# GraphSAGE layer ends: the last half in two groups of blocks, statistics gathered ahead, and the next layer's first h written by two engines

## The chip, the cores and the metric

The kernel runs on one core of one Trainium2 chip. A core has a matrix engine (PE; its weight loads are listed as PEld), a vector engine (DVE), a scalar engine (ACT), a general engine (POOL) and a queue engine that only starts transfers (SP). The matrix engine writes its results into PSUM, a memory[...], and transfers (DMA) go between SBUF and device memory. The metric is the device time of one execution in microseconds, as the median of several runs.

## The reference, cut to what matters

An attention layer comes first and is not touched. The second part is a three-layer GraphSAGE over 16 graphs of 1024 nodes with 128 features:

```python
def _sage(x, adj, Wr, Wx, b, mf):
    deg = jnp.clip(jnp.sum(adj, axis=-1, keepdims=True), 1.0, None)
    agg = jnp.einsum('bij,bjd->bid', adj, x) / deg
    out = agg @ Wr + x @ Wx + b
    nrm = jnp.maximum(jnp.linalg.norm(out, axis=-1, keepdims=True), NORM_EPS)
    return out / nrm * mf[..., None]

def _bn(x, g, b):
    m = jnp.mean(x, axis=(0, 1))
    v = jnp.var(x, axis=(0, 1))
    return (x - m) * jax.lax.rsqrt(v + BN_EPS) * g + b

h1 = _bn(jax.nn.relu(_sage(x, adj_d, Wr1, Wx1, b1, mf)), g1, be1)
h2 = _bn(jax.nn.relu(_sage(h1, adj_d, Wr2, Wx2, b2, mf)), g2, be2)
h3 = _bn(jax.nn.relu(_sage(h2, adj_d, Wr3, Wx3, b3, mf)), g3, be3)
xc = jnp.concatenate([h1, h2, h3], axis=-1) * mf[..., None]
return (xc @ Wl + bl) * mf[..., None]
```

`_bn` takes its mean and variance over all graphs and all nodes. So nothing of layer L + 1 can be computed before the last node of layer L is done, and the scale and shift of the batch norm ("affine") stand between the two layers.

## The kernel before, in words

Each layer goes through the 16 graphs `b`, and each graph through two halves `c` of 512 nodes (512 = 4 blocks of 128). One half is one call of the generator `nodes(L, b, c, hT, aT)`. Here `hT` is the layer's input, features on the partitions; `aT` the masked adjacency for this half; `ys[b % 2]` the product of the input with Wr, made by `given`.

A half goes like this. PE makes `own` = bias + h Wx, and ACT copies it into `mine` (L1123). Then for each of the four blocks `i`, PE adds up eight 128x128 products into `pg` (L1132). `pg` is one PSUM tile of shape [P, 2, 512], that is two banks: blocks 0 and 1 lie in the first bank, blocks 2 and 3 in the second. In layer 0 column 128 of each block carries the node degree. After the fourth block, DVE takes all four together: in layer 0 the degree and its reciprocal (L1143, L1146), then `o = pg * rdeg + mine`, one instruction for each block (L1150). ACT squares `o` (L1155), DVE adds the squares up per row (L1158) and bounds them (L1160), ACT takes the root (L1161), DVE the reciprocal, the mask and relu times 1/norm (L1163 to L1165). PE transposes the result into the bank `pt` (L1169), ACT copies it to `hTs[b]`, which stays in SBUF (L1173), and DVE takes batch-norm statistics of it (`bn_stats`, L1176, or L1172 in a layer's last half): mean and variance of 512 columns for each feature, one of 32 entries in `late["stats"]`.

The order of the instructions on PE, ACT and DVE is written out by hand: the block runs under `tc.manual_schedule`, and each of these engines executes in program order. The generator's `yield`s let the main loop interleave two halves: while PE makes the sums of half `this`, DVE and ACT do the steps "scaled", "norm", "result", "transposed" and "end" of the half `before` (L1256 to L1313). Beside them, DVE applies the dilation masks to the `aT` of the next half: four `pieces` of 1.2 us each, made by `masks` (L146). SP's and POOL's queues are filled by the scheduler. On SP stand the loads of `aT` (2 MB, four buffers) and of the mask's data `mr` (two of 0.5 MB for each half, four buffers); a load waits until its buffer is free, and holds what is queued behind it. On POOL stand the loads and stores of the output's accumulator (`sums_so_far` and L1069).

A tile that two engines access is guarded by semaphores that the framework sets. PSUM tiles come by tag: `bank` with "n" gives the one bank for `given`, "t" the one for transposes, "g" half of a two-bank tile out of the same two slots that `pg` uses.

At a layer's end (L1318 to L1336) nothing is left to interleave: the last half goes through "scaled" to "end" alone. In layers 1 and 2 PE has the output products of the previous layer for graphs 14 and 15 to do there (`last_parts`, 4 parts of 8 products; L1059), and DVE their 16 additions afterwards (L1064). Then `bn_aggr` joins the 32 entries (L1325), and six small operations give `affine` (L1328 to L1332). The next layer begins at L1220: ACT writes `h` of graph 0 in two halves (`incoming`, L1096), PE makes `given` for each (L1103; both use the bank "n", so the second waits for ACT's copy of the first, L1105), then `own` and the sums of the first half. After layer 2 the output loop follows (L1388 to L1406): `come` applies the last batch norm, `products` multiplies by Wl's third part (L1364), DVE and ACT add the rows to the accumulator (L1372, L1401, L1385), and SP stores the result. Its products for graphs with b % 4 < 2 go into one two-bank tile, for the others into two single banks (L1355 to L1359).

Of the kernel before, what the change touches and what calls it, by code (L numbers as in the profile page):

```python
# [10 lines left out]
F32 = mybir.dt.float32  # L11
# [4 lines left out]
AF = mybir.ActivationFunctionType  # L16
ALU = mybir.AluOpType
# [4 lines left out]
P = 128  # L22
LN_EPS = 1e-5
BN_EPS = 1e-5
NORM_EPS = 1e-12
# [9 lines left out]
def swept(ctx: ExitStack, tc: tile.TileContext, t: dict, out: bass.AP, flag: bass.AP):  # L35
# [8 lines left out]
    nc = tc.nc  # L44
    x, adj, nodemask = t["x"], t["adj"], t["nodemask"]
    B, N, D = x.shape
# [3 lines left out]
    HB = NB // 2  # L50
    HN = N // 2

    const = ctx.enter_context(tc.tile_pool(name="const", bufs=1))
# [7 lines left out]
    ident = const.tile([P, P], F32, name="ident")  # L61
# [17 lines left out]
    def last(ap, d):  # L79

        return ap.unsqueeze(2).to_broadcast([P, ap.shape[-1], d])
# [69 lines left out]


    mf2 = const.tile([P, B * NB], F32, name="mf2")
    bn_eps = const.tile([P, 1], F32, name="bn_eps")
    nc.vector.memset(bn_eps, BN_EPS)
    minus_half = const.tile([P, NB], F32, name="minus_half")
    nc.vector.memset(minus_half, -0.5)

# [931 lines left out]
    def incoming(L, b, c, hT, affine):  # L1090

        if L == 0:
            whole(incoming_first(L, b, c, hT))
        else:
            cc = slice(c * HN, (c + 1) * HN)
            nc.scalar.activation(hT[:, cc], hTs[b][:, cc], AF.Identity, bias=affine[:, 1:2], scale=affine[:, 0:1])  # L1096

    def given(L, b, c, hT, tag="n"):

        pn = bank(f"pn_{L}_{b}_{c}", tag).rearrange("p (k d) -> p k d", d=D)  # L1100
        for i in range(HB):
            n = (c * HB + i) * P
            nc.tensor.matmul(pn[:, i, :], hT[:, n : n + P], wts[f"Wr{L + 1}"], start=True, stop=True)  # L1103
        yield "evict"
        nc.scalar.copy(ys[b % 2][:, c * HB : (c + 1) * HB, :D], pn)  # L1105

    def nodes(L, b, c, hT, aT):

        y = ys[b % 2]
        k0 = b * NB + c * HB
        width = D + 1 if L == 0 else D
        own = bank(f"own_{L}_{b}_{c}", "o").rearrange("p (k d) -> p k d", d=D)
        start_with(own, 2 + L, P)
        for i in range(HB):
            n = (c * HB + i) * P
            nc.tensor.matmul(own[:, i, :], hT[:, n : n + P], wts[f"Wx{L + 1}"], start=False, stop=(i == HB - 1))
        yield "own"

        def evict():
            mine = late["pool"].tile([P, HB, D], F32, name=f"mine_{L}_{b}_{c}", tag="mine")
            nc.scalar.copy(mine, own)  # L1123
            return mine


        mine = evict() if late else None
        pg = ps_s.tile([P, 2, 512], F32, name=f"pg_{L}_{b}_{c}", tag="sc")
        for i in range(HB):
            for j in range(NB):  # L1130
                at = (i % 2) * (D + 1)
                nc.tensor.matmul(  # L1132
                    pg[:, i // 2, at : at + width], aT[:, j, i * P : (i + 1) * P], y[:, j, :width],
                    start=(j == 0), stop=(j == NB - 1),
                )
            yield "sums"
        if not mine:
            mine = evict()
            yield "mine"
        pool, small, rdeg = late["pool"], late["small"], late["rdeg"]  # L1140
        if L == 0:
            dg = rdeg[:, k0 : k0 + HB]
            nc.vector.tensor_scalar(  # L1143
                dg.rearrange("p (q i) -> p q i", q=2), pg[:, :, D : 2 * D + 2 : D + 1], 1.0, None, ALU.max
            )
            nc.vector.reciprocal(dg, dg)  # L1146
        o = pool.tile([P, HB, D], F32, name=f"o_{L}_{b}_{c}", tag="o")
# [17 lines left out]
        nc.vector.scalar_tensor_tensor(o, o, 0.0, last(f, D), ALU.max, ALU.mult)  # L1165
        yield "result"
        pt = bank(f"pt_{L}_{b}_{c}", "t")
        for i in range(HB):
            nc.tensor.transpose(pt[:, i * P : (i + 1) * P], o[:, i, :], ident)  # L1169
        last_half = b == B - 1 and c == 1  # L1170
        if last_half:
            nc.vector.bn_stats(late["stats"][:, 2 * b + c, :], pt)  # L1172
        nc.scalar.copy(hTs[b][:, c * HN : (c + 1) * HN], pt)  # L1173
        yield "transposed"
        if not last_half:
            nc.vector.bn_stats(late["stats"][:, 2 * b + c, :], pt)  # L1176
        yield "end"

    turns = [(L, b, c) for L in range(3) for b in range(B) for c in range(2)]

# [4 lines left out]
    def go(steps, *names):  # L1185
        for name in names:
            assert next(steps) == name


    late = {}  # L1190
    hTs = []
# [13 lines left out]
        late["rdeg"] = late["small"].tile([P, B * NB], F32, name="rdeg", bufs=1)  # L1205

    def new_stats(L):
        late["stats"] = late["small"].tile([P, 2 * B, 6], F32, name=f"stats{L}", tag="stats", bufs=2)

    p1 = ctx.enter_context(ExitStack())  # L1210
    affine = None
    with tc.manual_schedule(
# [3 lines left out]
        hT, last_rows = attend()  # L1216
        next(last_rows)
        nothing = lambda: None
        for L in range(3):
            if L > 0:  # L1220
                new_stats(L)
                hT = shared.tile([P, N], F32, name=f"h_{L}_0", tag="ad", bufs=2)
                for c in range(2):
                    incoming(L, 0, c, hT, affine)
                for c in range(2):
                    whole(given(L, 0, c, hT))
            before = None

            held, last_parts = ["o", "g", "g", "y"], []
            for b in range(B):  # L1230
# [4 lines left out]
                for c in range(2):  # L1235
# [49 lines left out]
                            next(last_rows)  # L1285
                    if biased:
                        next(biased)
                    turn_later = before and (c == 0 or L == 0)
                    if before and not turn_later:
                        go(before, "transposed")  # L1290
                    pieces[2]()
                    pieces[3]()
                    if before and not turn_later:
                        go(before, "end")
                    go(this, "sums")
                    if turn_later:
                        go(before, "transposed", "end")
# [17 lines left out]
                    fetch_h0(b + 2)  # L1315
                if more:
                    hT = hTn
            go(before, "scaled")  # L1318
            for part in last_parts[:2]:
                next(part)  # L1320
            go(before, "norm", "result", "transposed", "end")
            for part in last_parts[2:]:
                next(part)
            mv = late["small"].tile([P, 3], F32, name=f"mv{L}", tag="mv", bufs=2)
            nc.vector.bn_aggr(mv[:, 0:2], late["stats"])  # L1325

            affine = late["small"].tile([P, 2], F32, name=f"affine{L}", tag="affine", bufs=2)
            nc.scalar.activation(mv[:, 1:2], mv[:, 1:2], AF.Sqrt, bias=bn_eps)  # L1328
            nc.vector.scalar_tensor_tensor(mv[:, 2:3], mv[:, 0:1], -1.0, late["norms"][:, L, 0:1], ALU.mult, ALU.mult)
            nc.vector.reciprocal(mv[:, 1:2], mv[:, 1:2])  # L1330
            nc.vector.tensor_tensor(affine[:, 0:1], late["norms"][:, L, 0:1], mv[:, 1:2], ALU.mult)
            nc.vector.scalar_tensor_tensor(  # L1332
                affine[:, 1:2], mv[:, 2:3], mv[:, 1:2], late["norms"][:, L, 1:2], ALU.mult, ALU.add
            )
            for part in last_parts:
                whole(part)  # L1336

# [4 lines left out]
                nc.sync.dma_start(tile_[:, b], acc_d[1][4 * i + b])  # L1342
            outs.append(tile_)


        hs = {}

        def come(b):
            if b < B:
                hs[b] = shared.tile([P, N], F32, name=f"h_3_{b}", tag=("ad", "xin")[b % 2], bufs=2 + b % 2)  # L1350
                for c in range(2):
                    incoming(3, b, c, hs[b], affine)
# [625 lines left out]
```

## Time and profile before

| | |
|---|---|
| median of 3 runs | 3398.19 us (3393.63 to 3403.14) |
| profiled execution | 3396.91 us, span 3395.1 us |
| PE, DVE, ACT busy over the span | 98%, 89%, 68% |
| mean granted PE clock | 0.995 |
| DMA | 772.28 MB, mean 227 GB/s |
| last half of layers 0, 1, 2: sums end, affine ready | 2649.37, 2657.74; 2994.93, 3002.98; 3336.34, 3344.39 us |
| next layer's (or output's) first product of that kind | 2664.96; 3007.82; 3346.60 us |

Times are from the start of the span. "Granted clock" is the share of the full rate that the matrix engine was given. The three GraphSAGE layers lie from 2326 us to 3345 us of the span, and the three layer ends lie at about 2650, 2995 and 3336 us. In a timeline row, the numbers are start and length, then engine, source line, operation, output and input with sizes, how many instructions were merged, and in brackets how long the engine had been idle before it and which instruction ended the wait.

### The profile page before, as it was taken

The page shows a single profiled execution, that of the slowest core. Times are in us where ns is not written, and L with a number is a line of the kernel's source. Part 1 is how long each engine was busy: PE and PEld are TensorE (multiplying, and loading weights), DVE is VectorE, ACT ScalarE, POOL GpSimd, SP SyncE. Part 2 cuts the span into 40 slices and gives each one's busy share as a digit, 9 for nine tenths or more (in the row PEclk, how much of TensorE's full clock was granted, in tenths as well). Part 3 has the DMA queues.
Part 4 walks back from the last instruction along what each step waited for, and adds up shares of the span by engine and source line. Part 5 has one row for each costly group of instructions (what it writes and reads, how often), then busy time and mean ns, then how long its engine had stood idle before and what let it go on. Part 6 is the DMA issues. An engine that isn't in the chain of part 4 may idle for free. (4 is left out here: it accounts for less than half of the span.)

```text
span 3395.1 us, 86338 instructions
## 1 busy us (share of the span) xinstructions
PE 3310.6 (98%) x34855; PEld 1872.4 (55%) x34855; DVE 3025.5 (89%) x5399; ACT 2305.4 (68%) x3909; POOL 164.2 (5%) x253
## 2 busy tenths in 40 slices
PE   8999999999999999999999999999999899999997
PEld 3333333333333333333334334336999899999997
DVE  7898989989989998998998999897888899988887
ACT  7699689779879969968976986884232344423334
POOL 2000000000000000000000000000000000000000
PEclk9999999999999999999999999999999999999999
DMA  7357456547637736845863773677999799989996
GB/s 242 108 168 206 137 149 199 161 129 221 188 122 213 221 122 183 238 144 158 236 190 122 237 240 119 189 228 261 346 341 343 284 353 350 353 323 350 352 351 222
DMA packets 650123, 772.28 MB, mean 227 GB/s; under 512 B 173264, under 2 KB 569168, under 8 KB 637424
## 3 DMA queue, kind: packets, MB, share of 16 engines
q1 hardware_dynamic: 632672, 708.58, 64.4%
q0 software_dynamic: 15456, 57.30, 5.0%
q8 instruction: 275, 4.51, 0.6%
q14 instruction: 136, 1.11, 0.1%
q10 hardware_dynamic: 1584, 0.79, 0.1%
HBM read 508.50 MB, written 157.29 MB: 196 GB/s over the span
## 5 line engine op out<-in xcount | busy, mean ns | idle before, releaser
L603 DVE TENSOR_TENSOR w<-e,aT 128x1024 f32<-128x1024 f32 x1024 | 1205.5, 1219 | 138.4 <-ACT e L598 136.8
L598 ACT ACTIVATE e<-sc 128x1024 f32<-128x1024 f32 x1024 | 991.9, 1022 | 333.6 <-PE sc L560 332.6
L1132 PE MATMUL pg<-y,aT 128*128 128x128 f32 (+1 forms) x6144 | 729.8, 275 | 0.0
L1132 PEld LDWEIGHTS pg<-y,aT 128*128 128x128 f32 x6144 | 707.9, 192 | 0.0
L487 PE MATMUL acc<-w,both 128*32 128x512 f32 x4096 | 586.7, 605 | 3.1 <-DVE w L603 2.6
L560 PE MATMUL sc<-qT,kT 32*128 32x512 f32 x4096 | 584.4, 640 | 0.3 <-ACT qT L315 0.3
L492 PE MATMUL acc<-e,eps 128*32 128x512 f32 x4096 | 573.1, 592 | 0.0
L146 DVE SCALAR_TENSOR_TENSOR aT<-mr,aT 128x1024 f32<-128x1024 bf16 x384 | 458.8, 1217 | 0.0
L492 PEld LDWEIGHTS acc<-e,eps 128*32 128x32 f32 x4096 | 150.6, 110 | 294.6 <-issue 289.6
L1155 ACT ACTIVATE sq<-o 128x512 f32<-128x512 f32 x96 | 60.6, 631 | 328.5 <-DVE o L1150 328.5
L554 PEld LDWEIGHTS <-never 32*32 32x32 bf16 x8192 | 80.9, 88 | 347.9 <-issue 325.6
L554 PE MATMUL sc<-nomask,never 32*32 32x512 bf16 x8192 | 252.3, 385 | 16.8 <-ACT e L598 12.3
L1173 ACT COPY hT<-pt 128x512 f32<-128x512 f32 x96 | 56.3, 586 | 289.3 <-PE pt L1169 280.0
L560 PEld LDWEIGHTS sc<-qT,kT 32*128 32x128 f32 x4096 | 160.1, 183 | 116.9 <-issue 116.1
L505 PEld LDWEIGHTS pa<-ident,a 128*128 128x128 f32 x1024 | 107.7, 141 | 181.4 <-issue 129.7
L487 PEld LDWEIGHTS acc<-w,both 128*32 128x32 f32 x4096 | 92.8, 108 | 156.2 <-issue 65.4
L915 ACT ACTIVATE wr<-both,th 128x512 f16<-128x512 f16 x256 | 172.1, 730 | 7.1 <-DVE both L900 6.9
L505 PE MATMUL pa<-ident,a 128*128 128x128 f32 x1024 | 168.3, 287 | 6.4 <-DMA a<-in_adj 5.7
L512 ACT ACTIVATE nomask<-aT 128x512 bf16<-128x512 f32 x256 | 161.4, 630 | 8.1
L1150 DVE SCALAR_TENSOR_TENSOR o<-pg,rdeg,mine 128x128 f32<-128x128 f32 x384 | 108.1, 344 | 55.9 <-PE pg L1132 52.6
L508 ACT COPY aT<-pa 128x512 f32<-128x512 f32 x256 | 152.7, 597 | 5.3 <-PE pa L505 4.3
L900 DVE TENSOR_TENSOR_SCAN both<-rk 128x513 f16<-128x513 bf16 x128 | 155.9, 1218 | 0.0
(228 smaller groups left out, 3894.9 us busy)
## 6 DMA issues: line engine op xcount, KB each, us to landing
aT<-aT_d SPq DMA_DIRECT2D x94, 2048.0 KB, 9.9
mr<-mr_d SPq DMA_DIRECT2D x188, 512.0 KB, 6.0
aT_d<-aT SPq DMA_DIRECT2D x256, 256.0 KB, 4.0
a<-in_adj SPq DMA_DIRECT2D x253, 256.0 KB, 3.7
ad<-in_adj SPq DMA_DIRECT2D x112, 512.0 KB, 4.2
nomask<-nomask SPq DMA_DIRECT2D x512, 96.0 KB, 2.7
nomask<-nomask SPq DMA_DIRECT2D x512, 64.0 KB, 2.7
nomask<-nomask SPq DMA_DIRECT2D x512, 32.0 KB, 2.7
```

Source lines behind the costliest of these rows:

```text
L146: nc.vector.scalar_tensor_tensor(part, mrs[h][:, j : j + 2, :].rearrange("p j n -> p (j n)"), 0.0, part, ALU.is_equal, ALU.mult)
L487: nc.tensor.matmul(acc[g][32 * j : 32 * j + 32, :], v1[:, m, (2 * j + g) * HW : (2 * j + g) * HW + 32], ws[j // 2][:, j % 2, :], start=(m ...
L492: nc.tensor.matmul(acc[g][32 * j : 32 * j + 32, :], eps8, es[j // 2][:, j % 2, :], start=False, stop=(m == NB - 1),)
L505: nc.tensor.transpose(pa[:, k * P : (k + 1) * P], a[:, k, :], ident)
L512: nc.scalar.activation(nomask[:, 0, :], aT[:, 0, :], AF.Relu, bias=1.0, scale=-1e38, accum_out=zeros[:, i : i + 1])
L554: nc.tensor.matmul(scs[j // 2][to : to + 32, j % 2, :], never[rows, rows], nomask[rows, j, :], start=True, stop=False, tile_position=(32 * ...
L560: nc.tensor.matmul(scs[j // 2][:, j % 2, :], kT[rows, mm], qTs[c][rows, g, :], start=False, stop=True, tile_position=(32 * j, 0),)
L598: nc.scalar.activation(e, scs[q], AF.Exp, scale=1.0 / math.sqrt(HD))
L603: nc.vector.tensor_tensor(w, es[q], aT.to_broadcast([P, 2, HN]), ALU.mult)
L900: nc.vector.tensor_tensor_scan(pair_sums[b % 2], row[:, 0::2], row[:, 1::2], 0.0, ALU.add, ALU.add)
L915: nc.scalar.activation(wrs[b][:, t * HN : (t + 1) * HN], pair_sums[b % 2][:, t : t + HN], AF.Abs, bias=at[:, b : b + 1], scale=2.0,)
L1132: nc.tensor.matmul(pg[:, i // 2, at : at + width], aT[:, j, i * P : (i + 1) * P], y[:, j, :width], start=(j == 0), stop=(j == NB - 1),)
```

## The change

The last half of a layer (b = 15, c = 1) leaves the common path. A new generator `ending` takes its four blocks in two groups. The code of the first group (scale, square, norm, relu of blocks 0 and 1) is issued between the sums of block 1 and those of block 2; the scaling of block 2 between the sums of blocks 2 and 3; the rest after block 3. Squares and their sums are made on DVE by one instruction with an accumulator output, and in layer 0 the degree is taken for each block alone. The statistics of the last half go into two entries of their own (`late["two"]`). The 31 other entries are aggregated ahead of the last half's first group (`most`), and the two sets are joined by their weights, 31/32 and 1/32, after the last statistics.

The half before the last one is transposed, copied and put into the statistics before the last half's third block; and the masks `pieces[2:]` of the next half are kept (`owed`) and applied after the next layer's first h. That first h is written by `arrive`: two quarters by ACT, the second half by DVE. In layers 0 and 1 this stands at the head of the next layer, after the additions of `last_parts`; in layer 2 it stands ahead of them. At the end of layer 0, where there are no output products, PE makes 14 and 18 transposes of the identity that nobody reads (`running`).

```diff
+    def arrive(hT, b, affine):
+        for cc in (slice(0, HN // 2), slice(HN // 2, HN)):
+            nc.scalar.activation(hT[:, cc], hTs[b][:, cc], AF.Identity, bias=affine[:, 1:2], scale=affine[:, 0:1])
+        nc.vector.tensor_scalar(hT[:, HN:], hTs[b][:, HN:], affine[:, 0:1], affine[:, 1:2], ALU.mult, ALU.add)
...
             yield "sums"
+            if last_half and i == 1:
+                end = ending(L, k0, pg, mine)
+                go(end, "first group")
+            if last_half and i == 2:
+                go(end, "third block")
+        if last_half:
+            yield from end
+            return
...
+    def ending(L, k0, pg, mine):
...
+        def scaled(i):
+            at, dg = (i % 2) * (D + 1), rdeg[:, k0 + i : k0 + i + 1]
+            if L == 0:
+                nc.vector.tensor_scalar(dg, pg[:, i // 2, at + D : at + D + 1], 1.0, None, ALU.max)
+                nc.vector.reciprocal(dg, dg)
+            nc.vector.scalar_tensor_tensor(
+                o[:, i, :], pg[:, i // 2, at : at + D], dg, mine[:, i, :], ALU.mult, ALU.add
+            )
+            nc.vector.scalar_tensor_tensor(
+                sq[:, i, :], o[:, i, :], 1.0, o[:, i, :], ALU.mult, ALU.mult, accum_out=f[:, i : i + 1]
+            )
+
+        def root(two):
+            nc.vector.tensor_scalar(f[:, two], f[:, two], NORM_EPS**2, None, ALU.max)
+            nc.scalar.activation(f[:, two], f[:, two], AF.Sqrt)
+
+        def normed(two):
+            nc.vector.reciprocal(f[:, two], f[:, two])
+            nc.vector.tensor_tensor(f[:, two], f[:, two], mf[:, k0 + two.start : k0 + two.stop], ALU.mult)
+            nc.vector.scalar_tensor_tensor(o[:, two, :], o[:, two, :], 0.0, last(f[:, two], D), ALU.max, ALU.mult)
+
+        def turned(two):
+            for i in range(two.start, two.stop):
+                nc.tensor.transpose(pt[:, i * P : (i + 1) * P], o[:, i, :], ident)
+
+        def counted(two):
+            nc.vector.bn_stats(late["two"][:, two.start // 2, :], pt[:, two.start * P : two.stop * P])
+
+        first, second = slice(0, 2), slice(2, 4)
+        for i in range(2):
+            scaled(i)
+        root(first)
+        normed(first)
+        yield "first group"
+        scaled(2)
+        yield "third block"
+        pt = bank(f"pt_{L}_end", "t")
+        turned(first)
+        scaled(3)
+        root(second)
+        counted(first)
+        normed(second)
+        yield "result"
+        turned(second)
+        counted(second)
+        nc.scalar.copy(hTs[B - 1][:, HN:], pt)
+        yield "end"
+
+    def running(L, n):
+
+        idle = bank(f"idle_{L}_{n}", "n")
+        for i in range(n):
+            nc.tensor.transpose(idle[:, (i % HB) * P : (i % HB + 1) * P], ident, ident)
...
-                for c in range(2):
-                    incoming(L, 0, c, hT, affine)
+                arrive(hT, 0, affine)
+                for piece in owed:
+                    piece()
...
-                    turn_later = before and (c == 0 or L == 0)
+                    last_half = b == B - 1 and c == 1
+                    turn_later = before and (c == 0 or L == 0) and not last_half
...
+                    if last_half:
+                        owed = pieces[2:]
                         go(before, "end")
+                        most = late["small"].tile([P, 4], F32, name=f"most{L}", tag="most", bufs=2)
+                        nc.vector.bn_aggr(most[:, 0:2], late["stats"])
+                        nc.vector.tensor_scalar(most[:, 2:3], most[:, 0:1], SHARE, None, ALU.mult)
+                        nc.vector.tensor_scalar(most[:, 3:4], most[:, 1:2], SHARE, BN_EPS, ALU.mult, ALU.add)
...
-            go(before, "scaled")
+            go(before, "result")
             for part in last_parts[:2]:
                 next(part)
-            go(before, "norm", "result", "transposed", "end")
+            if L == 0:
+                running(L, 14)
+            go(before, "end")
             for part in last_parts[2:]:
                 next(part)
-            mv = late["small"].tile([P, 3], F32, name=f"mv{L}", tag="mv", bufs=2)
-            nc.vector.bn_aggr(mv[:, 0:2], late["stats"])
+            if L == 0:
+                running(L, 18)
+            mv = late["small"].tile([P, 5], F32, name=f"mv{L}", tag="mv", bufs=2)
+            gain, shift = late["norms"][:, L, 0:1], late["norms"][:, L, 1:2]
+            nc.vector.bn_aggr(mv[:, 0:2], late["two"])
+            nc.vector.tensor_tensor(mv[:, 2:3], mv[:, 0:1], most[:, 0:1], ALU.subtract)
+            nc.vector.scalar_tensor_tensor(
+                mv[:, 2:3], mv[:, 2:3], SHARE * (1.0 - SHARE), mv[:, 2:3], ALU.mult, ALU.mult
+            )
+            nc.vector.scalar_tensor_tensor(mv[:, 1:2], mv[:, 1:2], 1.0 - SHARE, mv[:, 2:3], ALU.mult, ALU.add)
...
-            nc.scalar.activation(mv[:, 1:2], mv[:, 1:2], AF.Sqrt, bias=bn_eps)
...
+            nc.scalar.activation(mv[:, 3:4], mv[:, 1:2], AF.Sqrt, bias=most[:, 3:4])
...
+            if L == 2:
+                hs[0] = shared.tile([P, N], F32, name="h_3_0", tag="ad", bufs=2)
+                arrive(hs[0], 0, affine)
             for part in last_parts:
                 whole(part)
...
-        come(0)
         come(1)
```

More of the change, by code (lines that the diff above doesn't have):

```diff
@@ L153, in swept @@
     mf2 = const.tile([P, B * NB], F32, name="mf2")
-    bn_eps = const.tile([P, 1], F32, name="bn_eps")
-    nc.vector.memset(bn_eps, BN_EPS)
     minus_half = const.tile([P, NB], F32, name="minus_half")
@@ L1169, in nodes @@
             nc.tensor.transpose(pt[:, i * P : (i + 1) * P], o[:, i, :], ident)
-        last_half = b == B - 1 and c == 1
-        if last_half:
-            nc.vector.bn_stats(late["stats"][:, 2 * b + c, :], pt)
         nc.scalar.copy(hTs[b][:, c * HN : (c + 1) * HN], pt)
         yield "transposed"
-        if not last_half:
-            nc.vector.bn_stats(late["stats"][:, 2 * b + c, :], pt)
+        nc.vector.bn_stats(late["stats"][:, 2 * b + c, :], pt)
         yield "end"
+    def ending(L, k0, pg, mine):
+        pool, small, rdeg = late["pool"], late["small"], late["rdeg"]
+        o = pool.tile([P, HB, D], F32, name=f"o_{L}_end", tag="o")
+        sq = pool.tile([P, HB, D], F32, name=f"sq_{L}_end", tag="sq")
+        f = small.tile([P, HB], F32, name=f"f_{L}_end", tag="f")
+        def scaled(i):
[40 more added lines that the diff above has]
+        yield "end"
@@ L1207, in new_stats @@
     def new_stats(L):
-        late["stats"] = late["small"].tile([P, 2 * B, 6], F32, name=f"stats{L}", tag="stats", bufs=2)
+        late["stats"] = late["small"].tile([P, 2 * B - 1, 6], F32, name=f"stats{L}", tag="stats", bufs=2)
+        late["two"] = late["small"].tile([P, 2, 6], F32, name=f"two{L}", tag="two", bufs=2)
     p1 = ctx.enter_context(ExitStack())
@@ L1218, in swept @@
         nothing = lambda: None
+        SHARE = 1.0 - 0.5 / B
+        hs = {}
         for L in range(3):
@@ L1287, in swept @@
                         next(biased)
-                    turn_later = before and (c == 0 or L == 0)
+                    last_half = b == B - 1 and c == 1
+                    turn_later = before and (c == 0 or L == 0) and not last_half
                     if before and not turn_later:
                         go(before, "transposed")
-                    pieces[2]()
-                    pieces[3]()
-                    if before and not turn_later:
+                    if last_half:
+                        owed = pieces[2:]
                         go(before, "end")
+                        most = late["small"].tile([P, 4], F32, name=f"most{L}", tag="most", bufs=2)
+                        nc.vector.bn_aggr(most[:, 0:2], late["stats"])
+                        nc.vector.tensor_scalar(most[:, 2:3], most[:, 0:1], SHARE, None, ALU.mult)
+                        nc.vector.tensor_scalar(most[:, 3:4], most[:, 1:2], SHARE, BN_EPS, ALU.mult, ALU.add)
+                    else:
+                        pieces[2]()
+                        pieces[3]()
+                        if before and not turn_later:
+                            go(before, "end")
                     go(this, "sums")
@@ L1317, in swept @@
                     hT = hTn
-            go(before, "scaled")
+            go(before, "result")
             for part in last_parts[:2]:
                 next(part)
-            go(before, "norm", "result", "transposed", "end")
+            if L == 0:
+                running(L, 14)
+            go(before, "end")
             for part in last_parts[2:]:
                 next(part)
-            mv = late["small"].tile([P, 3], F32, name=f"mv{L}", tag="mv", bufs=2)
-            nc.vector.bn_aggr(mv[:, 0:2], late["stats"])
@@ L1327, in swept @@
-            affine = late["small"].tile([P, 2], F32, name=f"affine{L}", tag="affine", bufs=2)
-            nc.scalar.activation(mv[:, 1:2], mv[:, 1:2], AF.Sqrt, bias=bn_eps)
[L1329 to L1334, printed above, removed]
+            if L == 0:
+                running(L, 18)
@@ new lines, in swept @@
+            affine = late["small"].tile([P, 2], F32, name=f"affine{L}", tag="affine", bufs=2)
+            nc.scalar.activation(mv[:, 3:4], mv[:, 1:2], AF.Sqrt, bias=most[:, 3:4])
+            nc.vector.scalar_tensor_tensor(mv[:, 4:5], mv[:, 0:1], 1.0 - SHARE, most[:, 2:3], ALU.mult, ALU.add)
+            nc.vector.scalar_tensor_tensor(mv[:, 4:5], mv[:, 4:5], -1.0, gain, ALU.mult, ALU.mult)
+            nc.vector.reciprocal(mv[:, 3:4], mv[:, 3:4])
+            nc.vector.tensor_tensor(affine[:, 0:1], gain, mv[:, 3:4], ALU.mult)
@@ L1335, in swept @@
+            nc.vector.scalar_tensor_tensor(affine[:, 1:2], mv[:, 4:5], mv[:, 3:4], shift, ALU.mult, ALU.add)
+            if L == 2:
+                hs[0] = shared.tile([P, N], F32, name="h_3_0", tag="ad", bufs=2)
+                arrive(hs[0], 0, affine)
             for part in last_parts:
@@ L1343, in swept @@
             outs.append(tile_)
-        hs = {}
         def come(b):
```

## The prediction

> **What bounds the kernel now.** I read first the busy times in stretches of 100 us over the GraphSAGE layers, then the timeline round each layer's end.
>
> ```profile
> 2500.00:2600.00 100.00, 100.00 (x891) 99.62 (x890) 84.01 (x160) 29.48 (x61) 2.65 (x5) 1.00 0.95 341
> 2600.00:2700.00 100.00, 91.04 (x780) 89.73 (x779) 79.04 (x154) 32.88 (x71) 1.61 (x3) 0.95 0.83 296
> 2900.00:3000.00 100.00, 96.20 (x850) 95.53 (x850) 89.53 (x167) 36.69 (x86) 3.73 (x7) 0.99 0.96 352
> ```
>
> The columns after the stretch are its length and the busy us of PE, PEld, DVE, ACT, POOL, then the granted clock, DMA share and GB/s. Inside a layer PE is busy 100 of 100 us, so a gap in PE is not made up later. Gaps exist only where a layer ends: the batch norm needs the last half's sums before the next layer's first product. The change touches exactly these three places, which I call ends 0, 1 and 2. End 0, from the timeline:
>
> ```profile
> 2645.63 0.69 DVE L1165 SCALAR_TENSOR_TENSOR o<-o,f 128x512 f32<-128x512 f32 x1
> 2646.98 0.60 PE L1169 MATMUL pt<-ident,o 128*128 128x128 f32 x4
> ...
> 2654.11 0.99 PE L1169 MATMUL pt<-ident,o 128*128 128x128 f32 x4 [4.74 <-DVE o L1165]
> 2655.13 0.70 DVE L1172 BATCH_NORM_STATS2 stats<-pt 128x6 f32<-128x512 f32 x1 [1.17 <-PE pt L1169]
> 2655.87 1.02 DVE L1325 BATCH_NORM_AGGREGATE mv<-stats 128x2 f32<-128x192 f32 x1
> ...
> 2657.53 0.21 DVE L1332 SCALAR_TENSOR_TENSOR affine<-mv,norms 128x1 f32<-128x1 f32 x1
> ...
> 2658.64 2.08 PE L1103 MATMUL pn<-weights,h 128*128 128x128 f32 x8 [3.54 <-ACT h L1096]
> ...
> 2661.39 2.08 PE L1103 MATMUL pn<-weights,h 128*128 128x128 f32 x8 [0.68 <-ACT y L1105]
> ...
> 2664.96 5.52 PE L1132 MATMUL pg<-y,aT 128*128 128x128 f32 x48
> ```
>
> Start, length, engine, line, in brackets the idle time and who ended it. The last sums end at 2649.37, affine is there at 2657.74, the next layer's sums start at 2664.96: 15.6 us. End 1 has the same chain from 2994.93 over 3002.98 to 3007.82; end 2 goes from 3336.34 over 3344.39 to the first output product at 3346.60. Half of end 0's products run at half speed, and the clock column says why:
>
> ```profile
> 2649.40:2654.00 4.60, 0.00 (x0) 0.00 (x0) 3.36 (x11) 0.83 (x2) 0.00 (x0) 1.00 1.02 368
> 2654.00:2656.00 2.00, 0.99 (x4) 0.61 (x4) 0.83 (x2) 0.13 (x1) 0.00 (x0) 0.56 0.98 410
> 2996.70:2999.20 2.50, 0.01 (x1) 0.00 (x0) 1.89 (x5) 0.32 (x2) 0.00 (x0) 0.96 0.83 321
> 2999.20:3001.20 2.00, 1.95 (x10) 1.98 (x10) 0.79 (x2) 0.09 (x1) 0.00 (x0) 0.50 1.01 434
> ```
>
> After 2.5 idle us PE works at 0.50 for about 3.3 us (until 3002.4 at end 1).
>
> **Who may touch a two-bank tile.** The split puts DVE's reads of pg between the matmuls that fill it. The trace of before has no such place, but the output loop has a tile of the same shape (both, [P, 2, 512]):
>
> ```profile
> 3349.90 1.12 DVE L1372 SCALAR_TENSOR_TENSOR outs<-py,mf,outs 128x128 f32<-128x128 f32 x4 [1.38 <-PE py L1364]
> 3351.14 0.63 ACT L1401 ACTIVATE tmp<-py,mf 128x128 f32<-128x128 f32 x2 [3.79 <-DVE outs L1372]
> ...
> 3355.49 0.62 ACT L1401 ACTIVATE tmp<-py,mf 128x128 f32<-128x128 f32 x2
> ```
>
> The four adds of L1372 read bank 0 only, yet begin when the 16th product is through (18 from 3346.60 took 3.69, so 16 end at 3349.9), not the eighth. ACT's L1401 reads bank 1 only, yet waits for those adds; this wait is counted 8 times, once for each of the 8 of 16 graphs whose halves share a tile, and not for those with two tiles (3355.49). So engines take turns on the whole tile. The Trainium skill (PSUM — Partial Sum Buffer, "PSUM bank collisions raise a hardware error") asks less: two engines must be kept apart in one bank, reads against reads too. Both speak against the change. By the row, matmuls of blocks 2 and 3 each wait for the DVE reads written ahead of them; by the page, only block 3's do (block 2 fills the other bank). I take the row and give the page's sum below.
>
> **The change, part by part.**
>
> *Half before, and statistics ahead.* Its result ends at 2646.32 at end 0. Its transposes move ahead of block 2's matmuls: PE is through with block 1 at 2641.62 + 32 x 0.1163 = 2645.34 and waits 1.1 us (end 1 already has this wait, 1.26; end 2 none, no masks there). Transposes until 2647.06, ACT's copy 0.59 + 0.04, and only then bn_stats, since one bank is read by turns (L1176 waits for L1173 in the trace): 2648.42. New bn_aggr over 186 values: L1325's 1.02 for 192 gives 1.00; two tensor_scalar 0.25. DVE reaches the first group at 2649.7, 3.4 after the result. The same at end 1 (2990.58 to 2994.0) and end 2 (3331.82 to 3335.4).
>
> *One block's "scaled".* Dependent small DVE operations stand 0.20 apart (L1330, L1331), a 128x128 STT 0.38 to a dependent one. The square moves from ACT (0.63) and the reduce (0.69) to a second STT with accum_out. Such an operation has a second instruction in the trace:
>
> ```profile
> L716 DVE DVE_READ_ACCUMULATOR rk<-rk,gl 128x1 f32 x112 | 9.2, 82 | 0.0
> ```
>
> So 0.38 + 0.28 + 0.08 = 0.74 per block; with the per-block degree (0.41) 1.15 in layer 0. Four blocks: 3.0 or 4.6 us against before's 1.54 + 0.75 + 0.72.
>
> *End 1 in sequence.* STT of block 1 done at 2994.0 + 0.74 + 0.34 = 2995.1. Block 2's 16 matmuls start only then; PE has idled 3.8 us, so they take 16 x 0.2225 + 0.1 (pitch of the slow products, L1103 at end 0): 2998.8. Block 2's STT 2999.15; block 3 warm, 1.95: 3001.15. Scaled(3) 0.9: 3002.05; max 0.2; counted(first), 128x256, lies between 0.281 (128) and 0.695 (512): 0.42, so 3002.7; reciprocal, multiply, STT 128x256 (0.46 between 0.34 and 0.69) 0.87: 3003.55. Before them PE did the first transposes and 16 output products (3003.4), so the second transposes end at 3004.0. counted(second) 0.46, bn_aggr of 12 values 0.24 (6 take 0.173): 3004.75. Three dependent operations 0.6, ACT's root 0.37, three more 0.49: affine at 3006.2, 3.2 later than before. Deferred masks' 2.35 us are off this path, but what replaced them is longer.
>
> *End 0*, same steps with 1.15 per block: block 2 starts 2651.6 (cold), 2655.3; block 3 2656.1 to 2658.05; affine 2663.5, 5.8 late. *End 2*, as end 1: 3335.4 + 12.2 = 3347.6, 3.2 late.
>
> *First h by two engines.* ACT's 128x256 lies between 0.39 (L1049) and 0.81 (L1096): 0.53, the second 0.44 on. DVE's half: fp32 tensor_scalar in SBUF took 0.22 for 128 and 0.68 for 1024 columns (L237, L988), so 0.42; the other bound is L429's 0.68. At end 0: h quarters 2664.1 and 2664.55, products warm thanks to the 14 + 18 idle transposes (2.1 us for 18, hidden in the wait), copy 0.63, second product 2665.6, and 2.11 more to the sums as at end 1 of before (3005.71 to 3007.82): 2667.7 against 2664.96, **+2.75**; the warm clock returns 3 of 5.8 us.
> At end 1 the code differs: the 16 adds of the last output parts (4.22, L1064) stand ahead of DVE's half of h. It comes at 3006.2 + 4.2 + 0.42 = 3010.85; the second product starts there, 3.2 us after the first ended. Cold it takes 3.57 to the sums (2661.39 to 2664.96), warm 2.11: 3014.45 or 3013.0, **+6.6** or +5.2. The Trainium skill (TensorE: Matmul & The Clock Gate, Part 1) has the clock fall after an idle window of about 3.4 us, which would leave this gap warm; the row shows 2.5 us enough, so I take +6.6.
> At end 2 the half comes ahead of the adds, and the first output product waits for the eighth add (its PSUM slot): 3347.6 + 0.42 + 2.15 = 3350.2 against 3346.60, **+3.6**. ACT's earlier h is covered by that wait.
>
> *Moved masks and queues.* Two masks (2.35) run after DVE's h: at end 0 by 2666.4, at end 1 by 3013.2, needed by the fifth of each 8 matmuls, half a microsecond into sums that start later: nothing. They release an mr buffer. SP's queue holds its load and, behind it, the next aT: at end 1 issued at about 3013 instead of 2993.2 and 2995, 18 us late, 3.5 MB with what follows, some 10 us at 350 GB/s: landed by 3024. That aT is masked two halves on (after 3033): hidden; uncovered it would cost up to its lateness. POOL's accumulator writes follow the adds, 3 to 4 us late; their reloads are needed over 10 us later.
>
> Sum: 2.75 + 6.6 + 3.6 = **+13.0**. The profiled execution took 3396.9 (span 3395.1 and 1.8 round it), 1.3 below the median; added to the median 3398.2: **3411**. By the page's banks block 2 is free, but block 3 waits for block 2's read behind the whole first group, PE by then 4 to 5 us idle: 0.3 better at each end, 3410.
>
> **Rivals.**
> - *Matmuls and reads of pg overlap* (the tile is not taken by turns). Sums end before 2651, 2995.1, 3336.2; only DVE's chain remains: -1.2, +1.6, +0.5, about 3399. Against: the eight waits. 0.10.
> - *Faster:* DVE keeps up, so that after the last sums only block 3's chain (5.3 instead of 8.2) remains: three ends -8.7, warm clock at end 0 -3.6, quarter h's -1: 3385. It decides if DVE is at the first group by block 1's end, 2645.4; I have it at 2649.7, with bn_stats behind ACT's copy and the aggregate ahead. 0.07.
> - *Clock stays low through block 3 as well* (0.9 and 0.4 us gaps restart the low time): 16 x 0.11 = 1.8 at each end, 3416. 0.15. For: at end 0 short gaps kept it at 0.50 for 10 us.
> - *Milder:* end 1's second product warm (-1.4), interpolated DVE operations at their lower bounds (-0.3 at each end), the clock back after half of block 2 (8 x 0.11 = 0.9 at each end): +8, 3406. 0.20. The forecast itself 0.48 (3408 to 3414).
>
> **Numbers.** A measurement of this kernel tells about 0.3%, 10.2 us, from no change. Slower: 0.15, the forecast less a tail 0.42, a little of the milder case 0.06: 0.63. Same: 0.10 + 0.14 + 0.06 = 0.30. Faster: 0.07. The range runs from the overlap case to past the low clock: 3395 to 3419; the forecast's own is 3406 to 3416.
>
> **What would show it.** Block 2's matmuls starting with the DVE STT of block 1, at half clock, after 3 to 5 idle us, and block 3's waiting on DVE again; affine 3 to 6 us later against the half before; at end 1 the second pn product waiting for DVE, behind L1064's adds. If pg's 64 matmuls run through without a DVE wait, the forecast falls.

## The result and the profile after

The changed kernel takes 3408.2 us in the median of 8 runs (3405.8 to 3410.1), against 3395.4 of 8 runs of the kernel before: ratio 1.0034, 95% interval 1.0023 to 1.0045, so 8 to 15 us slower (12.8 between the medians). The forecast was 13.0 us slower.

The stretches of 100 us of the changed kernel, with the same columns as before:

```profile
2500.00:2600.00 100.00, 100.00 (x891) 99.62 (x890) 83.79 (x161) 29.48 (x61) 2.64 (x5) 1.00 0.95 341
2600.00:2700.00 100.00, 91.48 (x790) 89.92 (x789) 82.05 (x176) 30.99 (x70) 1.60 (x3) 0.98 0.80 288
2900.00:3000.00 100.00, 94.75 (x818) 93.72 (x817) 86.58 (x172) 34.96 (x83) 3.72 (x7) 0.97 0.89 326
3000.00:3100.00 100.00, 96.05 (x823) 95.05 (x821) 82.93 (x178) 30.02 (x57) 5.87 (x11) 0.97 0.89 320
```

The last of these stretches in the kernel before:

```profile
3000.00:3100.00 100.00, 98.60 (x862) 97.85 (x861) 83.90 (x171) 31.60 (x58) 6.42 (x12) 0.99 0.89 324
```

Inside a layer PE is as busy as before. The losses are at the layer ends, and at end 1 most of all. The second row shows that busy time is no measure of the outcome: PE is busier there than before (91.48 against 91.04) and at a higher clock (0.98 against 0.95), but 3.8 us of it are the transposes that nobody reads. End 0 in the timeline of the changed kernel:

```profile
2640.98 0.69 DVE L1177 SCALAR_TENSOR_TENSOR o<-o,f 128x512 f32<-128x512 f32 x1
...
2641.81 0.63 PE L1181 MATMUL pt<-ident,o 128*128 128x128 f32 x4 [1.10 <-DVE o L1177]
2642.48 0.59 ACT L1182 COPY hT<-pt 128x512 f32<-128x512 f32 x1 [2.71 <-PE pt L1181]
2643.10 0.70 DVE L1184 BATCH_NORM_STATS2 stats<-pt 128x6 f32<-128x512 f32 x1 [1.43 <-ACT hT L1182]
2643.83 1.00 DVE L1369 BATCH_NORM_AGGREGATE most<-stats 128x2 f32<-128x186 f32 x1
...
2644.99 0.15 DVE L1197 TENSOR_SCALAR rdeg<-pg 128x1 f32<-128x1 f32 x1
...
2646.36 0.35 DVE L1199 SCALAR_TENSOR_TENSOR o_end<-pg,rdeg,mine 128x128 f32<-128x128 f32 x1
...
2646.76 3.46 PE L1136 MATMUL pg<-y,aT 128*128 128x129 f32 x16 [4.32 <-DVE o_end L1199]
...
2651.06 2.05 PE L1136 MATMUL pg<-y,aT 128*128 128x129 f32 x16 [0.83 <-DVE o_end L1199]
...
2657.95 0.21 DVE L1425 SCALAR_TENSOR_TENSOR affine<-mv,norms 128x1 f32<-128x1 f32 x1
...
2658.85 1.20 PE L1106 MATMUL pn<-weights,h 128*128 128x128 f32 x8 [0.87 <-ACT h L1098]
...
2662.83 5.52 PE L1136 MATMUL pg<-y,aT 128*128 128x128 f32 x48
```

Read it from DVE: the result of the half before ends at 2641.67, then come ACT's copy, bn_stats and the aggregate, DVE begins the first group at 2644.99 (L1197), and PE stands still for 4.32 us until DVE has read block 1 out of PSUM (`o_end`, L1199, done at 2646.71). Block 2 runs at half clock (3.46 for 16 products), then PE waits again for the read of block 2. How the clock followed, in stretches of the changed kernel's end 0 (the clock is the last but two):

```profile
2642.50:2646.70 4.20, 0.00 (x0) 0.00 (x0) 3.36 (x12) 0.56 (x1) 0.00 (x0) 0.95 0.62 237
2646.80:2650.00 3.20, 3.20 (x16) 3.20 (x16) 1.16 (x6) 0.20 (x1) 0.00 (x0) 0.54 0.00 0
2651.00:2653.00 2.00, 1.94 (x17) 1.95 (x18) 0.30 (x3) 0.00 (x0) 0.00 (x0) 1.00 0.00 0
```

The attention layer, which the change does not touch, was 4.65 us shorter in this profiled execution than in the one of before, so I count from the end of the half before's result, called R (2646.32, 2990.58, 3331.82 before; 2641.67, 2988.45, 3337.83 after). "Next" is the first sum of the next layer or, at end 2, the first output product.

| us after R | affine, end 0 / 1 / 2 | next, end 0 / 1 / 2 |
|---|---|---|
| before | 11.42 / 12.40 / 12.57 | 18.64 / 17.24 / 14.78 |
| changed | 16.49 / 15.65 / 15.17 | 21.16 / 24.36 / 17.96 |

The differences in "next" are 2.52, 7.12 and 3.18, together 12.82. At end 1 the first 48 products take 6.54 instead of 5.52, 1.02 more. From the first output product to the end of the span it is 49.01 instead of 48.50, 0.51 more. That is 14.35 in all; less the 4.65 of the attention layer it gives the difference of the two spans, 3404.8 - 3395.1 = 9.7. These are two single executions; the medians differ by 12.8. Nothing is lost between the ends: from the next sums to the following R it is 325.62 us in both kernels in layer 1.

### The profile page after: what moved, and what is told of

Its sections match the earlier page's. It is cut to its first block, busy times and chain, and to the rows that moved or that the text cites. A ratio compares the mean times of both kernels' runs of the same rounds, so it can differ in the third digit from the quotient of the medians.

```text
span 3404.8 us, 86465 instructions
## 1 busy us (share of the span) xinstructions
PE 3314.2 (97%) x34887; PEld 1878.4 (55%) x34887; DVE 3034.1 (89%) x5464; ACT 2302.4 (68%) x3909; POOL 164.0 (5%) x253
## 4 chain that ended last, share of the span: by engine, by line
PE 65%; DVE 18%; ACT 9%; DMA 5%; issue 2%; SPq 1%; ACTq 0%; POOL 0%; DVEq 0%; POOLq 0%
PE pg L1136 20%; PE sc L558 9%; PE acc L485 8%; DVE w L601 8%; PE acc L490 7%; ACT e L596 4%; PE sc L552 3%; PE pn L1106 2%; PE own L1122 2%; DMA nomask<-nomask 2%; PE pa L503 2%; PE py L1057 1%; PE pt L1181 1%; DVE both L898 1%; DVE er L922 1%
## 5 line engine op out<-in xcount | busy, mean ns | idle before, releaser
L552 PE MATMUL sc<-nomask,never 32*32 32x512 bf16 x8192 | 249.9, 385 | 16.8 <-ACT e L596 12.8
```

Of the source, the lines that this page charges most:

```text
L552: nc.tensor.matmul(scs[j // 2][to : to + 32, j % 2, :], never[rows, rows], nomask[rows, j, :], start=True, stop=False, tile_position=(32 * ...
```

## The experiments

All are edits of the changed kernel, but for the seventh. Each ratio is to runs of the kernel before on the same chip, where its median was 3399.05 us (experiments 1 to 4) or 3396.46 us (5 to 8): compare the ratios, 1.0034 for the changed kernel, and not the times. The us after R are from one profiled execution of each.

### 1. The first h ahead of the additions

```diff
+            hs[0] = shared.tile([P, N], F32, name=f"h_{L + 1}_0", tag="ad", bufs=2)
+            arrive(hs[0], 0, affine)
+            for piece in owed:
+                piece()
             for part in last_parts:
                 whole(part)
```

(at all three ends; the same lines at the head of the layer are gone)

> Changed kernel with one edit: in layers 0 and 1 too, the next layer's first h and the two kept masks are issued ahead of the 16 additions of the last output parts (as the changed kernel has it after layer 2 alone). Theory (DVE's half of h stands behind the additions, and PE goes cold in the wait): at end 1 the second pn product follows ACT's copy of the first, about 2.6 us after affine instead of 4.7, warm; from the result of the half before to the next sums 24.4 falls to about 20.3, and the next 48 products take 5.5 instead of 6.5: 5 us in all, ends 0 and 2 unchanged, 3403. Rival (the additions hold up nothing, the first sums wait for masks or for y anyway): end 1 stays within 1 us of 24.4 and the time near 3408.

Measured: 3404.4 us, ratio 1.0017 (1.0009 to 1.0024). End 1 of the changed kernel, then of this one:

```profile
3004.02 4.22 DVE L1062 SCALAR_TENSOR_TENSOR acc<-py,mf,acc 128x128 f32<-128x128 f32 x16
...
3004.79 1.21 PE L1106 MATMUL pn<-weights,h 128*128 128x128 f32 x8 [1.04 <-ACT h L1098]
...
3008.16 0.53 DVE L1099 TENSOR_SCALAR h<-hT,affine 128x512 f32<-128x512 f32 x1
...
3008.84 2.04 PE L1106 MATMUL pn<-weights,h 128*128 128x128 f32 x8 [2.84 <-DVE h L1099]
...
3012.81 6.54 PE L1136 MATMUL pg<-y,aT 128*128 128x128 f32 x48
```

```profile
3010.73 0.55 DVE L1099 TENSOR_SCALAR h<-hT,affine 128x512 f32<-128x512 f32 x1
...
3011.38 1.20 PE L1106 MATMUL pn<-weights,h 128*128 128x128 f32 x8 [1.05 <-ACT h L1098]
...
3013.26 1.16 PE L1106 MATMUL pn<-weights,h 128*128 128x128 f32 x8 [0.68 <-ACT y L1108]
...
3015.74 5.56 PE L1136 MATMUL pg<-y,aT 128*128 128x128 f32 x48
```

The second pn group waits 0.68 us for ACT's copy instead of 2.84 for DVE, and is warm (at full clock; "cold" is half clock). Next sums come 20.74 after R instead of 24.36, and with the 48 products at 5.56 instead of 6.54 end 1 gains 4.6, as expected (5). So 4.6 of the loss come from one order of instructions at one end. The ends that this edit leaves alone did not stay the same, contrary to the expectation: end 0 was 2.1 us later, since blocks 2 and 3 both took 3.81, and end 2 1.5 earlier, since block 2 took 2.05. This is the clock; more on it below.

### 2. The last half's sums in two one-bank tiles

```diff
-        pg = ps_s.tile([P, 2, 512], F32, name=f"pg_{L}_{b}_{c}", tag="sc")
+        if last_half:
+            pgs = [bank(f"pg0_{L}", "g")] * 2 + [bank(f"pg2_{L}", "g")] * 2
+        else:
+            pg = ps_s.tile([P, 2, 512], F32, name=f"pg_{L}_{b}_{c}", tag="sc")
+            pgs = [pg[:, i // 2, :] for i in range(HB)]
```

> Changed kernel, the last half's pg as two tiles of one bank each (blocks 0 and 1, blocks 2 and 3) instead of one tile of two banks. Theory (whole tile by turns, PE idles till DVE has read block 1): block 2's sums now follow the transposes with no wait for DVE; block 3's still wait for the read of block 2, which comes behind the first group, PE then 3.5 to 4 us idle and cold, so block 3 takes 3.5 instead of 2.05 to 2.46; affine only 0.5 to 1 us earlier at each end, 3406. Rival (turns were by bank all along, the wait in block 2 has another cause): block 2 still waits 3.5 us and nothing changes, 3408.

Measured: 3405.9 us, ratio 1.0022 (1.0013 to 1.0032). Blocks 2 and 3 at end 1 of the changed kernel, then of this one:

```profile
2992.76 3.79 PE L1136 MATMUL pg<-y,aT 128*128 128x128 f32 x16 [3.54 <-DVE o_end L1199]
...
2996.99 2.46 PE L1136 MATMUL pg<-y,aT 128*128 128x128 f32 x16 [0.44 <-DVE o_end L1199]
```

```profile
2989.00 1.95 PE L1140 MATMUL pg<-y,aT 128*128 128x128 f32 x16
...
2994.60 3.78 PE L1140 MATMUL pg<-y,aT 128*128 128x128 f32 x16 [3.65 <-DVE o_end L1203]
```

Block 2 now follows the transposes at once; the wait of 3.54 us that it had with one tile of two banks is gone, so that wait belonged to the tile and not to the bank (one [P, 512] half of it). Block 3, whose bank DVE still reads, waits 3.65 instead, and is the cold one. Affine comes 16.24, 15.47 and 13.08 after R: 0.25 and 0.2 earlier at ends 0 and 1 (0.5 to 1 was expected), and 2.1 at end 2, where block 3 ran warm (2.05) after the same gap. At end 0 the next sums came 1.4 later all the same (22.55 after R), since the second pn group ran cold there (1.91).

### 3. Three one-bank tiles

As before, with block 3 in a bank of its own:

```diff
+            pgs[3] = bank(f"pg3_{L}", "y")
```

> Changed kernel, the last half's pg as three tiles of one bank: blocks 0 and 1, block 2, block 3 (in the bank of tag y). No DVE read stands between matmuls of one tile. Theory (PE's waits on DVE and the cold block cost what lies between this and the changed kernel; behind it DVE's own chain remains): block 2 and 3 follow without wait, affine about 3.4, 4 and 4 us earlier at ends 0, 1, 2 (from the result of the half before: 13.1, 11.6, 11.6), 3397. Rival (DVE's chain alone sets affine, the matmul waits are hidden behind it): affine less than 1 us earlier, 3406 to 3408.

Measured: 3396.3 us, ratio 0.9994 (0.9985 to 1.0003). The sums in one row at end 1, and PE's first transposes waiting for DVE after them:

```profile
2987.75 3.74 PE L1141 MATMUL pg<-y,aT 128*128 128x128 f32 x32
...
2993.17 0.41 PE L1222 MATMUL pt_end<-ident,o_end 128*128 128x128 f32 x2 [1.69 <-DVE o_end L1218]
```

Affine is at 12.58, 11.02 and 11.18 after R, 3.9, 4.6 and 4.0 earlier than in the changed kernel (expected 3.4, 4 and 4). This one edit takes back the whole loss: its interval includes 1. What remains is 1.4 and 0.8 gained at ends 0 and 2 against the kernel before, and 2.5 (and 0.3 in the sums) lost at end 1, where the additions still stand ahead of h.

### 4. Idle transposes in the gap

```diff
                     if last_half:
+                        running(L, 30)
                         owed = pieces[2:]
```

> Changed kernel plus 30 transposes of the identity that nobody reads, on PE in the gap between the transposes of the half before and block 2's sums, at all three ends. Theory (block 2 is slow because PE went cold in the gap): the start of block 2 stays, its 16 products take about 2.05 instead of 3.46 to 3.79, affine about 1.4 us earlier at each end, 3404. Rival (block 2 is slow for another reason, such as its operands' reads or a DVE access beside it): block 2 stays at 3.5 to 3.8, 3408 or later.

Measured: 3402.5 us, ratio 1.0015 (1.0006 to 1.0024). Its end 1:

```profile
2995.68 3.44 PE L1246 MATMUL idle<-ident 128*128 128x128 f32 x30
...
2999.39 2.05 PE L1136 MATMUL pg<-y,aT 128*128 128x128 f32 x16 [0.27 <-DVE o_end L1199]
```

Block 2 starts where it did (R + 4.32) and takes 2.05 instead of 3.79; at ends 0 and 2 it also takes 2.05. Affine is 1.4, 2.1 and 1.5 earlier. So of the 3.9 to 4.6 us that the waits cost at each end (experiment 3), 1.4 to 2.1 are the clock that falls in them.

### 5. The half before's statistics after block 2

```diff
-                        go(before, "end")
-                        most = ...
...
+                    if last_half:
+                        go(before, "transposed")
...
                     go(this, "sums")
+                    if last_half:
+                        go(before, "end")
+                        most = ...
```

(the transposes go behind block 2's sums; bn_stats, the aggregate and the two scalings behind DVE's scaling of block 2)

> Changed kernel with one part moved back: the half before is transposed and copied after block 2's sums, and its bn_stats and the aggregate of the 31 entries come after DVE's scaling of block 2, so DVE begins the first group right at the result of the half before. Theory (DVE is late for the first group because of ACT's copy, bn_stats and the aggregate ahead of it, and that is what PE waits for): block 2's sums start 1.8 us after that result at end 0 and 1.1 at ends 1 and 2, instead of 5.1, 4.3 and 4.5; affine about 12.1, 10.8 and 10.8 us after it instead of 16.5, 15.7 and 15.2; some 13 us faster than the changed kernel, near the kernel before (ratio about 1.0003). Rival (the work is only moved to a place where it is as much in the way, between block 2 and block 3): affine within 1.5 us of the changed kernel's, ratio above 1.0025.

Measured: 3395.0 us, ratio 0.9995 (0.9986 to 1.0003). Its end 1:

```profile
2981.84 0.69 DVE L1177 SCALAR_TENSOR_TENSOR o<-o,f 128x512 f32<-128x512 f32 x1
2982.45 0.34 DVE L1199 SCALAR_TENSOR_TENSOR o_end<-pg,rdeg,mine 128x128 f32<-128x128 f32 x1
...
2983.45 2.05 PE L1136 MATMUL pg<-y,aT 128*128 128x128 f32 x16 [2.03 <-DVE o_end L1199]
...
2985.94 2.05 PE L1136 MATMUL pg<-y,aT 128*128 128x128 f32 x16
...
2986.59 0.70 DVE L1184 BATCH_NORM_STATS2 stats<-pt 128x6 f32<-128x512 f32 x1 [0.37 <-ACT hT L1182]
```

DVE starts the first group at R, and block 2 starts 0.92 after R instead of 4.31. Affine: 12.95, 10.55 and 11.18 (expected 12.1, 10.8, 10.8). End 0 is later than expected because block 2, after a gap of 2.65, still took 2.86, and block 3 took 2.41. With one tile of two banks, too, the loss is gone, though block 2 still waits for DVE (2.65, 2.03 and 1.04 us). So the tile costs as much as it does because DVE comes late, and DVE comes late because the statistics of the half before were put ahead of the first group.

### 6. No idle transposes at end 0

The two `running` calls are taken out.

> Changed kernel without the 14 and 18 transposes that nobody reads at the end of layer 0. Theory (they keep PE at full clock through the wait for affine): the two pn groups take about 2.1 us each instead of 1.2, and with own the next sums start 2.5 us later after affine (7.2 instead of 4.7), ratio about 0.0007 higher than the changed kernel's 1.0034. Rival (the gaps of 2 to 3 us left without them are too short to lower the clock): no change at end 0.

Measured: 3411.0 us, ratio 1.0044 (1.0028 to 1.0059). End 0:

```profile
2660.35 2.07 PE L1106 MATMUL pn<-weights,h 128*128 128x128 f32 x8 [2.83 <-ACT h L1098]
...
2663.10 2.08 PE L1106 MATMUL pn<-weights,h 128*128 128x128 f32 x8 [0.68 <-ACT y L1108]
```

From affine to the next sums it is 24.27 - 16.83 = 7.4 us, against 4.7 with them: they are worth 2.8 us. The ratio moved by 0.0010 where 0.0007 was expected, but its interval (4 runs) overlaps with the changed kernel's: the gain is shown by the trace and not by the time.

### 7. The kernel before with the idle transposes alone

```diff
+            if L == 0:
+                running(L, 32)
             go(before, "norm", "result", "transposed", "end")
             for part in last_parts[2:]:
                 next(part)
+            if L == 0:
+                running(L, 18)
```

> Kernel before plus one part of the change alone: 32 and 18 transposes that nobody reads on PE at the end of layer 0, after the last sums and after the last transposes. Theory (cold clock costs end 0 about 2.5 us): the last transposes 0.6 instead of 1.0, the two pn groups 1.2 instead of 2.1 each, next sums 15.8 to 16.3 us after the result of the half before instead of 18.6, ratio about 0.9992. Rival (the idle transposes delay the real ones or the pn bank): next sums at 18.6 or later, ratio 1.000 or above.

Measured: 3392.2 us, ratio 0.9988 (0.9980 to 0.9997). The first pn group at end 0, and the second at end 1:

```profile
2653.96 1.16 PE L1103 MATMUL pn<-weights,h 128*128 128x128 f32 x8 [1.58 <-ACT h L1096]
...
2998.20 2.08 PE L1103 MATMUL pn<-weights,h 128*128 128x128 f32 x8 [0.68 <-ACT y L1105]
```

At end 0 the next sums come 15.89 after R instead of 18.64: 2.75 us gained. The part helps alone. At end 1, which the edit leaves as it was, the second pn group fell to half clock and the next sums came at 18.33, 1.1 later than before.

### 8. The three edits together

Three tiles, late statistics and the first h ahead of the additions.

> Changed kernel with the three edits together: three one-bank tiles for the last half's sums, late statistics of the half before, and the first h with its two masks ahead of the additions. Theory (what the change lost were PE's waits on DVE's reads, DVE's late start and the additions ahead of h; without them its shorter tail shows): affine 11.3, 9.7 and 9.7 us after the result of the half before, next sums or output products at 16.0, 14.8 and 12.5 instead of 18.6, 17.2 and 14.8 in the kernel before: 7 us faster than that, ratio 0.998. Rival (the gains overlap, DVE's own chain is the same sum of work): affine no earlier than with three tiles alone (12.6, 11.0, 11.2), ratio 0.999 or above.

Measured: 3388.4 us, ratio 0.9975 (0.9965 to 0.9985), the furthest ahead of the kernel before (experiment 7 is the other one whose interval lies below 1). Its end 1:

```profile
2982.54 0.69 DVE L1182 SCALAR_TENSOR_TENSOR o<-o,f 128x512 f32<-128x512 f32 x1
...
2984.18 1.95 PE L1141 MATMUL pg<-y,aT 128*128 128x128 f32 x16
...
2992.53 0.21 DVE L1430 SCALAR_TENSOR_TENSOR affine<-mv,norms 128x1 f32<-128x1 f32 x1
...
2995.31 1.16 PE L1106 MATMUL pn<-weights,h 128*128 128x128 f32 x8 [0.68 <-ACT y L1108]
```

Affine comes 11.07, 9.51 and 10.13 after R, next at 15.74, 14.55 and 12.92: 2.9, 2.7 and 1.9 earlier than in the kernel before, 7.5 in sum (expected 7). At end 0 almost all of it is the idle transposes: experiment 7 has affine at 11.05 and next at 15.89 there. So what the two groups and the early aggregate are worth by themselves shows at ends 1 and 2 only; in layer 0 each block costs DVE 0.99 us instead of 0.59 (its degree is taken by itself), which is part of the reason, and no run separates the rest. The edits overlap: experiments 3 and 5 each take back about 12.5 us in "next", yet together with the 4.6 of experiment 1 they give 21.3 and not 29.6, since 3 and 5 remove the same waits.

## Why the prediction was right, point by point

The mechanism came as forecast. That 13.0 and 12.8 agree to 0.2 us is in part luck: the parts below missed by up to 0.7 us in both directions, two costs (1.02 and 0.51 us) were not in the sum, and the measured difference is only known to lie between 8 and 15 us.

**DVE late for the first group.** Forecast 3.4 after R; measured 3.32, 3.32, 3.49. The chain of transposes, copy, bn_stats and aggregate is in the rows as worked out, and experiment 5 shows that it is the cause.

**Turns on the whole tile.** Block 2 waited for the read of block 1 at all three ends (4.32, 3.54, 3.55), block 3 for that of block 2 (0.83, 0.44, 0.44). Experiment 2 tells the row from the page of the Trainium skill (PSUM — Partial Sum Buffer, "PSUM bank collisions raise a hardware error"), by which only accesses to one bank must be kept apart: with separate tiles the wait in another bank is gone, with one tile it is there. The estimate that this difference matters little (0.3 at each end) held for affine at ends 0 and 1, because the wait then moves to block 3.

**Cold block 2.** Forecast 3.66, measured 3.46, 3.79, 3.53; that the gap causes it is shown by experiment 4. At end 2 it need not have come: in experiment 1 the same block after the same gap (3.54) took 2.05.

**Affine.** Forecast 5.8, 3.2 and 3.2 late, measured 5.07, 3.25 and 2.60. What I had too high is one block's "scaled": 0.59 apart instead of 0.74, and 0.99 instead of 1.15 in layer 0, since the accumulator's read (0.08) lies beside the square's end instead of behind it, and the next scaling starts with that read:

```profile
2992.15 0.29 DVE L1202 SCALAR_TENSOR_TENSOR sq_end<-o_end 128x128 f32<-128x128 f32 x1
2992.36 0.08 DVE L1202 DVE_READ_ACCUMULATOR sq_end<-o_end 128x1 f32 x1
2992.36 0.35 DVE L1199 SCALAR_TENSOR_TENSOR o_end<-pg,rdeg,mine 128x128 f32<-128x128 f32 x1
```

These rows are of the changed kernel's end 1. There block 3 took 2.46 instead of 1.95, the clock not yet back, which hid this.

**The ends.** +2.75, +6.6, +3.6 forecast, +2.52, +7.12 (and 1.0 in the 48 slow products, a cost that I left out: I had the clock back at the first sums), +3.18 measured. At end 1 I chose +6.6 over +5.2 because a gap of 3.2 us would be long enough for half clock; the gap was 2.84, the second product did run at half clock (2.04), and the last section shows why the length alone does not decide this. DVE's half of h took 0.53 to 0.55 instead of the 0.42 that I interpolated, between the two bounds (one of the two rows I interpolated between, L988, reads bf16 and not fp32); it is small against the additions ahead of it.

**Moved masks and queues.** Nothing, as forecast, but on other grounds. I had the next aT queued behind the late mr on SP, 18 us late. In the changed kernel SP's queue at end 1 has them the other way round:

```profile
2999.48 0.33 SPq L133 DMA_DIRECT2D aT<-aT_d  x1
3010.99 0.36 SPq L137 DMA_DIRECT2D mr<-mr_d  x1
```

SP's order is the scheduler's, not the program's, and it put aT first.

**The rivals.** "Matmuls and reads overlap" was priced 0.9 us above the kernel before, and experiment 3 builds it: ratio 0.9994, 2 us below. The low clock through block 3 came only in part in the changed kernel's profile (2.46 at end 1), but in full in experiment 1's end 0 (3.81 twice). "Faster" had its deciding point right (DVE at the first group in time) and its price too high: with that alone (experiment 5) the kernel is level with the one before, and with the other two edits it gains 7.5 in the profile, not 13. In that trace (experiment 8) DVE works from R to affine (9.5 to 11.1 us) with no wait longer than 0.54 us, so its own operations are then the chain.

## What to carry to other kernels

Work that is put ahead of a critical chain to shorten it must have idle time to lie in: here 1.25 us of aggregate and scalings and a bn_stats behind a copy were put just where DVE had become the engine that PE waits for, and they cost more than they saved. Before interleaving reads and matmuls of one PSUM tile, look for a tile of the same shape in the trace and see who waits for whom; separate tiles made the waits disappear. And when an operation is moved to another engine, read the whole queue ahead of it: the faster second half of h stood behind sixteen additions.

## What the runs showed of the hardware that was not expected

I took it from the trace of before that 2.5 idle us bring PE's clock down. They may or may not. After gaps of the same length at the same place the clock was found in either state: block 2 after 3.54 or 3.55 us took 3.79 and 3.53 in the changed kernel but 2.05 in experiment 1's end 2; block 3 after 3.65 took 3.78 at end 1 and 2.05 at end 2 of experiment 2; the last transposes after 2.54 took 1.08 in the kernel before and 0.63 in experiment 7.

The Trainium skill (TensorE: Matmul & The Clock Gate, Part 1) has a free-running window of about 3.4 us over which activity is judged. The traces here show it: in each of the ten, every change of the granted clock lies on one fixed grid of 3.413 us, and the low times at the layer ends last 3.41, 6.83 or 10.24 us, that is one, two or three windows. Here is the gap of 2.54 us at end 1 in two windows of the kernel before, then in two of experiment 7 (PE's busy time follows the comma, the clock is the last but two):

```profile
2995.57:2998.98 3.41, 1.14 (x11) 0.95 (x9) 2.28 (x8) 0.84 (x2) 0.00 (x0) 1.00 0.96 306
2998.98:3002.39 3.41, 3.14 (x15) 3.17 (x16) 2.01 (x4) 0.81 (x2) 0.00 (x0) 0.50 0.79 336
```

```profile
2987.82:2991.23 3.41, 1.83 (x17) 1.64 (x15) 2.23 (x8) 0.84 (x2) 0.00 (x0) 1.00 1.04 338
2991.23:2994.64 3.41, 2.41 (x20) 2.25 (x20) 2.50 (x4) 0.59 (x1) 0.00 (x0) 1.00 0.91 384
```

In the kernel before nearly all of the gap (2996.71 to 2999.25) falls into one window, and the next one is at half clock; in experiment 7 a window's edge cuts the gap, and the clock stays until a later window (2994.64 to 2998.05, 1.16 us busy) brings it down and slows the second pn group. Over all windows of the ten traces from 2326 us to the last 9 us, those at full clock with PE busy for 1.38 us or less were followed by half clock (30 of 30), those with 1.46 to 1.87 us by either (8 of 21 by half), those with 1.91 us or more never (2983). A window at half clock was followed by another with up to 2.74 us busy (21 of 21) and by full clock from 2.83 us on (38 of 38). The page has the clock fall after an idle window; here a window with up to 1.38 us of work in it was enough. Since the grid lies differently in each execution, a gap of this length has a price between nothing and 1.8 us for each 16 products of this kind (3.81 against 2.05), and a profile shows one draw of it. This also bounds what a single profile of such a kernel can say: the ends 0 and 2 of experiment 1 differ by +2.1 and -1.5 us where nothing was edited.
